# Row sums of the first adjacency: sixteen matmuls in the second network replaced by eight ScalarE sums in the first

## The chip, the cores and the metric

One Trainium2 chip, one core. The kernel is one program on that core; the metric is the device time of one execution in microseconds (us), median of several runs. The kernel before takes 1796.18 us (median of 3 runs, 1793.61 to 1801.1).

## What is computed

Sixteen graphs (batches) of 1024 nodes with 128 features, each with a symmetric 0/1 adjacency matrix, go through two networks, each on a layer-normed and rectified input and with a residual sum. Cut to what matters:

```python
# first network: 4 gated layers, each batch by itself
hw = h @ weight[i]
m  = einsum('bjn,bjd->bnd', adj, hw)          # aggregate
h  = gru_cell(m, h, ...)                      # sigmoid, sigmoid, tanh gates
# second network: 4 convolutions with a batch norm over all batches and nodes
h  = relu(einsum('bnm,bmc->bnc', adj, h @ W[i]) + b[i])
mu, var = mean(h, axis=(0, 1)), var(h, axis=(0, 1))
h  = gamma[i] * (h - mu) * rsqrt(var + 1e-5) + beta[i]
```

The batch norm is an affine map `sc * h + sh` per channel, whose two factors are known only when all sixteen batches of the layer before are done. For batch 0 the kernel does not wait for them: it aggregates the raw features, `adj @ h`, and puts the affine map in afterwards. Since `adj @ (sc*h + sh) = sc*(adj @ h) + sh*(row sums of adj)`, it needs the row sums of the adjacency of batch 0, called `degree`, as one row of 1024 numbers that stands in all 128 partitions.

## The kernel before, in words

The program tests whether the input is exact in a shorter format and runs `exact_path`; `general_path` is the other branch and does not run here.

**First network (about 0 to 1175 us).** Two streams, `sa` (batches 0, 2, 4, ...) and `sb` (1, 3, 5, ...), work in turn. One `half_step(one, two)` (L1035) interleaves the gates of `two` (`gate_step`, L955: 24 matmul instructions at L972) with the aggregation of `one` (`agg_step`, L933, 32 matmuls at L525). Half-steps are counted by `clock`; the first one that is called has the number 3. Tiles of a batch's adjacency stand in SBUF as eight `row` tiles (128 x 1024, fp32r) for all four layers of the batch. Work that is not part of the two streams is put in an agenda with `at(n, place, go)` and comes out in half-step n at one of several places: "late" (L1065) behind the first sigmoid (`first_act`) of the second half of the gates, "gap" (L1078) behind the last gate operation and the split, "mid" and others. `behind` sets only an order on one engine's own queue. From half-step 5 on, the order on TensorE, GpSimd and the DMA queue of SyncE is the written one, and a scheduler orders VectorE and ScalarE within these bounds. In half-step 8 `fetch` (L846) loads the adjacency of batch 2 into `stage` tiles (L573), `glance` (L581) sums their low halves on ScalarE (L587, one sum per tile into a column of `low`), and GpSimd rounds them into new `row` tiles (L578). After a gate step, features go out to DRAM and come back with blocks turned (`cross_h`, L591; `n_h`, L598), and are split in two parts, `ghw` (L905 on ScalarE, L906 on VectorE), which the next aggregation reads.

On GpSimd's DMA queue in half-step 7: a one-column copy that sets the pace (L1054), the 2 MB store of the turned adjacency of batch 1 (L623), and next the rounding casts of half-step 8 (L578).

**Second network (about 1174 to 1780 us).** Per layer and batch: eight loads of the stored bf16 adjacency on the queue of SyncE (L1232), eight casts to `wide` tiles (L1235 on ScalarE, L1237 on VectorE), 32 matmuls at L525. In layer 0 the features y come through GpSimd's queue (L1292) and are split into `chw` (L1294 on ScalarE, L1295 on VectorE); the weights come after the aggregation (`first_weights`, L1298: copy to `cm`, L1304 on ScalarE; matmuls L1305; `conv_done`, L1281). `raw_weights` (L1315) uses `degree` at L1322 once in each of the layers 1, 2 and 3.

`row_sums` (L1326) makes `degree` in layer 0, after the aggregation of batch 0: for each of the eight `wide` tiles and each half, one matmul with a 128 x 128 tile of ones (`ones_r`, made at L1372) as the weights, at L1331, into two PSUM tiles of the pool with two; all 128 rows of the result are the same. Two ScalarE copies (L1335) bring them to `degree`, which lies in `w_mT`, weights that the first network no longer needs.

Of the kernel before, what the change touches and what calls it, by code (L numbers as in the profile page):

```python
# [8 lines left out]
F32 = mybir.dt.float32  # L9
F32R = mybir.dt.float32r  # L10
BF16 = mybir.dt.bfloat16
U16 = mybir.dt.uint16
I32 = mybir.dt.int32
AF = mybir.ActivationFunctionType
ALU = mybir.AluOpType
AX = mybir.AxisListType
P = 128
HALF = 512
# [323 lines left out]
def exact_path(  # L342
# [21 lines left out]
    nc = tc.nc  # L364
    B, N, C = x.shape
    L = g_weight.shape[0]
    NB = N // P
    NH = N // HALF
# [3 lines left out]
    const = ctx.enter_context(tc.tile_pool(name="const", bufs=1))  # L372
    small = ctx.enter_context(tc.tile_pool(name="small", bufs=2))
    dram = ctx.enter_context(tc.tile_pool(name="dram", bufs=1, space=bass.MemoryType.DRAM))
# [7 lines left out]
    def tmp(name):  # L382
        return ps_t.tile([P, HALF], F32, tag="tmp", name=name)

    adjT_d = [dram.tile([NB, P, N], BF16, tag=f"adjT{b}", name=f"adjT_d{b}") for b in range(B)]
    xmid_d = [dram.tile([N, C], F32, tag=f"xmid{b}", name=f"xmid_d{b}") for b in range(B)]
    ymid_d = [dram.tile([P, N], F32, tag=f"ymid{b}", name=f"ymid_d{b}") for b in range(B)]

    def flat(name):
        return keep.tile([P, NB, C], F32, tag="x", name=name, bufs=4)  # L390
# [18 lines left out]
    ones = const.tile([P, 1], F32, tag="ones", name="ones")  # L409
    nc.vector.memset(ones, 1.0)  # L410
    low = const.tile([P, (B + 2) * NB], F32, tag="low", name="low")
    nc.vector.memset(low, 0.0)

    w_c = const.tile([P, L, C], F32, tag="w_c", name="w_c")
    w_mT = const.tile([P, L, 3 * C], F32, tag="w_mT", name="w_mT")
# [50 lines left out]
    def turn_layer(prep, w_g, i):  # L466

        pt = tmp(f"pt_whh{i}")
        for g in range(3):
            nc.tensor.transpose(pt[:, g * P : (g + 1) * P], wns["hh", i][:, g, :], ident)  # L470
        nc.scalar.copy(w_hhT[:, i, :], pt[:, : 3 * P])
        pt = tmp(f"pt_wih{i}")
        for g in range(3):
            nc.tensor.transpose(pt[:, g * P : (g + 1) * P], wns["ih", i][:, g, :], ident)

        w_ihT = prep.tile([P, 3 * C], F32, tag="w_ihT", name=f"w_ihT{i}", bufs=1)
        nc.scalar.copy(w_ihT, pt[:, : 3 * P])
        pg = tmp(f"pt_g{i}")
        nc.tensor.transpose(pg[:, :P], w_g[:, i, :], ident)
        w_gT = prep.tile([P, P], F32, tag="w_gT", name=f"w_gT{i}", bufs=1)  # L480
        nc.scalar.copy(w_gT, pg[:, :P])
        turned[i] = w_gT, w_ihT

    def join_layer(i):
        w_gT, w_ihT = turned[i]
        pw = tmp(f"pt_wm{i}")
        nc.tensor.matmul(pw[:, : 3 * P], w_gT, w_ihT, start=True, stop=True)
        nc.scalar.copy(w_mT[:, i, :], pw[:, : 3 * P])
# [45 lines left out]
    with ExitStack() as st:  # L534
        work = st.enter_context(tc.tile_pool(name="work", bufs=2))
# [45 lines left out]
        def glance(b, stage, js):  # L581

            junk = work.tile([P, N], BF16, tag="junk", name=f"junk{b}_{js[0]}", bufs=1)
            for j in js:
                lows = stage[j % 4].bitcast(U16).rearrange("p (n t) -> p n t", t=2)[:, :, 0]
                k = b * NB + j
                nc.scalar.activation(junk, lows, AF.Copy, accum_out=low[:, k : k + 1])  # L587

        def exchange_out(t, name):
            d = rawd.tile([P, HALF], F32, tag="cross", name=f"cross_{name}", bufs=8)  # L590
            nc.sync.dma_start(d, t)  # L591
            return d
# [19 lines left out]
        def transposes(batches):  # L612

            for b, rows in batches:
                adjT = turned_tile(f"adjT{b}")
                ahead = transpose_rows(b, rows[0], 0, adjT)
                for j in range(NB):
                    go = ahead
                    if j + 1 < NB:
                        ahead = transpose_rows(b, rows[j + 1], j + 1, adjT)  # L620
                    go()
                    yield j
                nc.gpsimd.dma_start(adjT_d[b].rearrange("k p n -> p k n"), adjT)  # L623
                yield NB
# [136 lines left out]
        def behind(*inss):  # L761

            es = ExitStack()
            for ins in () if written[0] else inss:
                es.enter_context(tc.issue_after(ins.ins))
            return es
# [261 lines left out]
        def at(n, place, go):  # L1028
            agenda.setdefault((n, place), []).append(go)

        def due(place):
            for go in agenda.pop((clock[0], place), ()):
                go()

        def half_step(one, two, gated=None, halfway=None):  # L1035

            feed.next_step()
            one.split = []
            if one.i == 0:
                two.fetch()  # L1040
            due("ins")
            if one is sb and one.i == 0 or written[0] and one is sa:
                feed.jobs = transposes([(s.b, s.rows) for s in (sa, sb)])
            if one.i > 0:
                one.split_step()
                two.fetch()
                feed.some(2)
            two.gate_step(0)
            two.half_away(0)
            two.first_four()  # L1050
            if feed.full or (clock[0], "mid") in agenda:

                pace = small.tile([P, 1], F32, tag="pace", name=f"pace{clock[0]}")
                nc.gpsimd.tensor_copy(pace, two.new[:, :1])  # L1054
                feed.store()
                due("mid")
            due("outs")
            one.split_back(0, two.last_act, two.mid_dve)
            one.split_back(1, two.last_act, two.mid_dve)
            if one.i > 0:  # L1060
                feed.some(1)
            two.gate_step(1, None, one.split)
            two.half_away(1)
            with behind(two.first_act):
                due("late")  # L1065
            if one.i == 0:
                feed.some(1)
            two.last_four()
            if gated:
                gated()  # L1070
            if one.i == 0:
                with behind(two.last_m):
                    one.split_step()
            one.agg_step(0)
            if halfway:
                halfway()
            with behind(two.last_act, two.last_dve, *one.split):
                due("gap")  # L1078
            feed.some(NB if written[0] and one is sa else 1)
            one.agg_step(1)  # L1080
            two.finish()
            clock[0] += 1

        sa, sb = Stream(0), Stream(1)
        every = {getattr(mybir.EngineType, e) for e in ("PE", "DVE", "Activation", "Pool", "SP")}
        with tc.tile_pool(name="prep", bufs=1) as prep, tc.manual_schedule(engines=every):
# [22 lines left out]
            late = [[work.tile([P, N], F32, tag="h", name=f"first{j}", bufs=7)] for j in range(4, NB)]  # L1109
# [83 lines left out]

            sa.plan(0)
            sb.plan(1)
            half_step(sa, sb, looks, lambda: turn_layer(prep, w_g, 1))
            join_layer(1)
            half_step(sb, sa, None, lambda: turn_layer(prep, w_g, 2))
# [25 lines left out]
    work = ctx.enter_context(tc.tile_pool(name="work2", bufs=2))  # L1224
# [65 lines left out]
    def first_split(b):  # L1290
        yt = flat(f"y{b}").rearrange("p k c -> p (k c)")
        nc.gpsimd.dma_start(yt, ymid_d[b])  # L1292
        hw = hw_tiles(b, f"chw{b}_0")
        nc.scalar.copy(hw[0], yt)  # L1294
        nc.vector.tensor_sub(hw[1], yt, hw[0].bitcast(F32))  # L1295
        return hw
# [26 lines left out]
            nc.tensor.matmul(pc[hf], w_c[:, i, :], mt[:, cols], start=True, stop=True)  # L1323
        conv_done(0, i, pc, stats)

    def row_sums(rows):  # L1326

        pd = [tmp(f"pt_deg{hf}") for hf in range(NH)]
        for j in range(NB):
            for hf in range(NH):  # L1330
                nc.tensor.matmul(  # L1331
                    pd[hf], ones_r, rows[j][:, hf * HALF : (hf + 1) * HALF], start=(j == 0), stop=(j == NB - 1)
                )
        for hf in range(NH):
            nc.scalar.copy(degree[:, hf * HALF : (hf + 1) * HALF], pd[hf])  # L1335

    xo = []

    def pieces(b):
# [28 lines left out]
            for n0, n in pieces(k):  # L1368
                nc.gpsimd.dma_start(xo_piece(k, n0, n), by_node(xmid_d[k], n0, n))

    ones_r = work.tile([P, P], F32R, tag="ones_r", name="ones_r", bufs=1)
    nc.vector.tensor_copy(ones_r, ones.to_broadcast([P, P]))  # L1372
    degree = w_mT.rearrange("p l c -> p (l c)")[:, :N]

    stats = small.tile([P, B * NH, 6], F32, tag="bn_st", name="stats0")
# [1 line left out]
    for b in range(B):  # L1377
        rows = load_adjT(b, 0)
        hw_next = first_split(b + 1) if b + 1 < B else None
        pm = banks(b, 0)  # L1380
        aggregate(pm, hw, rows, 0)
        if waiting:
            last = first_weights(*waiting, stats)
            if b == 1:
                with tc.issue_after(last.ins):
                    sb.rest()
        if b == B - 1:
            hw_next = raw_split(1)
        aggregate(pm, hw, rows, 1)
        if b == 0:  # L1390
            row_sums(rows)
        hw, waiting = hw_next, (b, pm)


# [1 line left out]
    for i in range(1, L):  # L1396
        rows, pm0, hw0 = load_adjT(0, i), banks(0, i), hw
# [8 lines left out]
        for b in range(1, B):  # L1406
            rows = load_adjT(b, i)
# [28 lines left out]
    for b in range(B):  # L1436
# [3 lines left out]
        for n0, n in pieces(b):  # L1440
# [5 lines left out]
            tag = turns[count % len(turns)]  # L1446
# [60 lines left out]
```

## Time and profile before

| what | value |
|---|---|
| runs shown | 1793.61, 1796.18, 1801.1 us; median 1796.18 |
| the profiled execution | 1796.9 us, of which 1795.0 us span |
| mean granted TensorE clock of it | 0.997 |
| TensorE busy | 98% of the span |
| VectorE, ScalarE, GpSimd busy | 70%, 62%, 22% |

In the page, TensorE stands as PE (matmuls) and PEld (weight loads), VectorE as DVE, ScalarE as ACT, GpSimd as POOL, SyncE's DMA queue as SPq. A line of a timeline gives the start in us from the start of the span, the duration in us, the engine, the line of the kernel, the operation, output <- inputs, shape, count, and in brackets how long the engine sat idle before it and who ended that. A line of a table by stretches gives the busy time of each engine in a stretch of the span, the granted clock, the mean share in which the 16 DMA engines were busy, and their rate.

### The profile page before, as it was taken

The numbers are of one execution on the slowest core, as the hardware profiler recorded it, in microseconds if no ns is written. First come the engines' busy times: TensorE is split into PE (matmuls) and PEld (weight loads), VectorE is DVE, ScalarE is ACT, GpSimd is POOL, SyncE is SP. The second block draws the span as 40 slices with busy tenths as digits, with TensorE's granted clock in tenths as the row PEclk, the third lists the DMA queues.
The fourth block names the chain that finished last, engine by engine and source line by source line (L and its number), as shares of the span: only waits on it lengthen the run. The fifth ranks groups of instructions, "written<-read, shape, count | busy, mean of one in ns | idle before, by whom it ended". The sixth has DMA issues, their size and how long they took to land. (4 is left out here: it accounts for less than half of the span.)

```text
span 1795.0 us, 22286 instructions
## 1 busy us (share of the span) xinstructions
PE 1763.4 (98%) x6742; PEld 1194.0 (67%) x6742; DVE 1258.8 (70%) x2308; ACT 1107.2 (62%) x1717; POOL 389.4 (22%) x417
## 2 busy tenths in 40 slices
PE   9999999999999999999999999999999999999997
PEld 6555565556565556556556555677778888888886
DVE  7567867867776776777786776676666666666665
ACT  5346456556556555755655655477777767768765
POOL 4213322332332331422342333110100000000011
PEclk9999999999999999999999999999999999999999
DMA  7448676776676766766767667778866566767667
GB/s 253 112 125 268 171 223 237 200 207 225 205 211 211 236 191 193 263 197 168 263 185 209 241 194 209 268 277 299 284 223 244 209 244 215 246 223 240 241 220 263
DMA packets 363968, 399.11 MB, mean 222 GB/s; under 512 B 159820, under 2 KB 240496, under 8 KB 363840
## 3 DMA queue, kind: packets, MB, share of 16 engines
q1 hardware_dynamic: 343088, 322.54, 57.1%
q0 software_dynamic: 20224, 74.80, 11.5%
q8 instruction: 55, 0.90, 0.2%
q14 instruction: 73, 0.60, 0.1%
q10 hardware_dynamic: 528, 0.26, 0.0%
HBM read 266.95 MB, written 96.99 MB: 203 GB/s over the span
## 5 line engine op out<-in xcount | busy, mean ns | idle before, releaser
L525 PE MATMUL pm<-row,ghw 128*128 128x512 f32 x2048 | 505.6, 403 | 11.8 <-ACT ghw L905 11.1
L525 PEld LDWEIGHTS pm<-row,ghw 128*128 128x128 f32 x2048 | 384.3, 189 | 124.5 <-issue 26.5
L525 PE MATMUL pc_m<-wide,chw 128*128 128x512 f32 x1024 | 246.1, 396 | 0.0
L609 POOL CAST half<-row 128x1024 bf16<-128x1024 f32 x128 | 148.8, 1171 | 327.2 <-DMA adjT<-half 312.5
L525 PEld LDWEIGHTS pc_m<-wide,chw 128*128 128x128 f32 x1024 | 190.5, 188 | 42.3 <-issue 4.3
L991 ACT ACTIVATE z<-g_z,brz 128x512 f32<-128x512 f32 x128 | 87.5, 684 | 171.3 <-PE g_z L972 171.2
L525 PE MATMUL pc_g_r<-wide,chw 128*128 128x512 f32 x464 | 187.0, 403 | 0.3 <-ACT chw L502 0.3
L578 POOL CAST row<-stage 128x1024 fp32r<-128x1024 f32 x112 | 131.5, 1181 | 243.6 <-DMA stage<-in_adj_dram 221.1
L525 PE MATMUL pc_g_z<-wide,chw 128*128 128x512 f32 x464 | 181.0, 390 | 0.0
L985 DVE SCALAR_TENSOR_TENSOR r<-g_hn,vecs,r 128x512 f32<-128x512 f32 x128 | 95.0, 742 | 118.3 <-ACT r L984 76.6
L1237 DVE CAST wide<-block 128x1024 fp32r<-128x1024 bf16 x160 | 109.8, 692 | 73.2 <-PE pc_m L525 46.2
L1237 DVE CAST wide<-packed 128x1024 fp32r<-128x1024 bf16 x160 | 110.2, 691 | 72.1 <-PE pc_g_z L525 53.9
L944 ACT COPY m<-pm 128x512 f32<-128x512 f32 x128 | 68.5, 586 | 147.9 <-PE pm L525 147.9
L990 ACT ACTIVATE r<-r,vecs 128x512 f32<-128x512 f32 x128 | 91.8, 717 | 104.0 <-DVE r L986 104.0
L997 DVE TENSOR_TENSOR h<-h,r 128x512 f32<-128x512 f32 x96 | 81.8, 852 | 101.6 <-ACT r L990 101.6
L1235 ACT CAST wide<-packed 128x1024 fp32r<-128x1024 bf16 x96 | 100.6, 1048 | 59.1 <-PE pc_m L525 28.3
L972 PE MATMUL g_r<-m,w_mT 128*128 128x512 f32 x256 | 131.5, 595 | 2.8 <-ACT m L944 2.3
L1235 ACT CAST wide<-block 128x1024 fp32r<-128x1024 bf16 x96 | 100.6, 1049 | 52.3 <-PE pc_g_z L525 27.7
L972 PE MATMUL g_xn<-m,w_mT 128*128 128x512 f32 x256 | 130.7, 592 | 0.0
L972 PE MATMUL g_z<-m,w_mT 128*128 128x512 f32 x256 | 130.7, 592 | 0.0
L998 DVE TENSOR_TENSOR h<-h,z 128x512 f32<-128x512 f32 x128 | 118.7, 931 | 4.8 <-ACT z L991 1.9
L1285 DVE BATCH_NORM_STATS2 stats<-feat 128x6 f32<-128x512 f32 x128 | 84.1, 686 | 47.0 <-ACT feat L1284 45.9
(187 smaller groups left out, 2804.3 us busy)
## 6 DMA issues: line engine op xcount, KB each, us to landing
block<-adjT_d SPq DMA_DIRECT2D x256, 256.0 KB, 4.7
packed<-adjT_d SPq DMA_DIRECT2D x256, 256.0 KB, 5.5
stage<-in_adj_dram SPq DMA_DIRECT2D x120, 512.0 KB, 4.8
adjT_d<-adjT POOLq DMA_DIRECT2D x16, 2048.0 KB, 8.3
cross_h<-t_h SPq DMA_DIRECT2D x90, 256.0 KB, 3.2
n_h<-cross_h SPq DMA_DIRECT2D x360, 64.0 KB, 2.0
xmid_d<-x POOLq DMA_DIRECT2D x16, 512.0 KB, 5.4
y<-ymid_d POOLq DMA_DIRECT2D x16, 512.0 KB, 5.9
```

Source lines behind the costliest of these rows:

```text
L525: nc.tensor.matmul(pm[hf], hw[s][:, j * P : (j + 1) * P], rows[j][:, hf * HALF : (hf + 1) * HALF], start=(j == 0 and s == 0), stop=(j == N ...
L578: nc.gpsimd.tensor_copy(t, stage[j % 4])
L609: nc.gpsimd.tensor_copy(t, row.bitcast(F32))
L972: nc.tensor.matmul(po, wT[:, i, g * C : (g + 1) * C], rhs, start=start, stop=stop)
L985: nc.vector.scalar_tensor_tensor(r, phn, b_hn(i), r, ALU.add, ALU.mult)
L990: nc.scalar.activation(r, r, AF.Tanh, bias=b_in(i))
L991: self.last_act = nc.scalar.activation(z, pz, AF.Sigmoid, bias=brz[:, 3 * i + 1 : 3 * i + 2])
L997: nc.vector.tensor_sub(ho, hin, r)
L998: nc.vector.tensor_mul(ho, ho, z)
L1235: nc.scalar.copy(r, t)
L1237: nc.vector.tensor_copy(r, t)
L1285: nc.vector.bn_stats(stats[:, b * NH + hf, :], dst)
```

## The change

The sums of the eight `row` tiles of batch 0 are taken by ScalarE in the first network, one activation (a copy with a sum along the free axis) for each tile, at eight places of the half-steps 5, 6 and 7. A new place "early" is put behind the first sigmoid of the first half of the gates. In the gap of half-step 7 GpSimd's queue stores the 128 x 8 sums to a row of 1024 numbers in DRAM; in the second network, where `row_sums` stood, GpSimd's queue loads that row into all 128 partitions of `degree`. The matmuls, their tile of ones and the two copies are gone. Since the matrix is symmetric, sums along rows and columns are the same.

```diff
+    degree_d = dram.tile([1, N], F32, tag="degree", name="degree_d")
...
+    deg = const.tile([P, NB], F32, tag="deg", name="deg")
...
+        def row_sums(rows, js):
+
+            junk = work.tile([P, N], BF16, tag="junk", name=f"total{js[0]}", bufs=1)
+            for j in js:
+                nc.scalar.activation(junk, rows[j].bitcast(F32), AF.Copy, accum_out=deg[:, j : j + 1])
...
             two.gate_step(0)
+            with behind(two.first_act):
+                due("early")
             two.half_away(0)
...
             sa.plan(0)
             sb.plan(1)
+            places = [(n, place) for n in (5, 6) for place in ("early", "late", "gap")] + [(7, "early"), (7, "late")]
+            for j, (n, place) in enumerate(places):
+                at(n, place, lambda j=j: row_sums(sa.rows, [j]))
+            at(7, "gap", lambda: nc.gpsimd.dma_start(degree_d.rearrange("o (k p) -> p (o k)", p=P), deg))
...
-    def row_sums(rows):
-
-        pd = [tmp(f"pt_deg{hf}") for hf in range(NH)]
-        for j in range(NB):
-            for hf in range(NH):
-                nc.tensor.matmul(
-                    pd[hf], ones_r, rows[j][:, hf * HALF : (hf + 1) * HALF], start=(j == 0), stop=(j == NB - 1)
-                )
-        for hf in range(NH):
-            nc.scalar.copy(degree[:, hf * HALF : (hf + 1) * HALF], pd[hf])
...
-    ones_r = work.tile([P, P], F32R, tag="ones_r", name="ones_r", bufs=1)
-    nc.vector.tensor_copy(ones_r, ones.to_broadcast([P, P]))
...
         if b == 0:
-            row_sums(rows)
+            nc.gpsimd.dma_start(degree, degree_d.rearrange("o n -> (o n)").partition_broadcast(P))
```

## The prediction

> **What bounds the kernel now.** I read first the busy times and the slices of the page, then tables by stretches over the two places that the change touches, then the timelines of TensorE and ScalarE there. The page, first part and the row of PE in 40 slices:
>
> ```profile
> PE 1763.4 (98%) x6742; PEld 1194.0 (67%) x6742; DVE 1258.8 (70%) x2308; ACT 1107.2 (62%) x1717; POOL 389.4 (22%) x417
> ...
> PE   9999999999999999999999999999999999999997
> ```
>
> TensorE has work nearly everywhere, so a matmul that goes is time that goes, unless the next input is late. All waits of TensorE in the trace's list sum to some 21 us; the largest, 11.1 us in 7 waits, is for `ghw` (L905), features on their way back through DRAM, all after 200 us.
>
> The stretches of half-steps 5 to 8 (each starts with its gates):
>
> ```profile
> 85.50:103.00 17.50, 17.50 (x58) 10.52 (x57) 11.97 (x30) 4.78 (x7) 4.90 (x6) 1.00 0.52 128
> 103.00:120.60 17.60, 17.60 (x58) 10.59 (x57) 12.28 (x32) 7.76 (x12) 3.83 (x5) 1.00 0.61 142
> 120.60:138.20 17.60, 17.60 (x57) 10.58 (x57) 10.17 (x18) 11.93 (x22) 1.08 (x2) 1.00 0.45 159
> 138.20:155.80 17.60, 17.60 (x57) 10.57 (x56) 10.56 (x16) 14.15 (x27) 7.09 (x6) 1.00 0.83 270
> ```
>
> The columns after the length are PE, PEld, DVE, ACT, POOL, clock, DMA share, GB/s. TensorE fills all of it at full clock; ScalarE is busy 4.8, 7.8 and 11.9 us of 17.6 where the sums go.
>
> **What is removed.** The timeline of TensorE around the old row sums:
>
> ```profile
> 1185.37 0.39 PE L525 MATMUL pc_g_r<-wide,chw 128*128 128x512 f32 x1
> 1185.78 3.89 PE L1331 MATMUL pt_deg<-wide,ones_r 128*128 128x512 f32 x16
> 1189.51 0.39 PE L525 MATMUL pc_g_z<-wide,chw 128*128 128x512 f32 x1
> ```
>
> A matmul is listed with 0.39 us but they overlap: neighbours at L525 start 0.23 us apart. From 1185.37 to 1189.51 are 4.14 us; without the 16 they would be 0.23. So 3.91 us of TensorE go, not 16 x 0.39 = 6.2. They stand in the middle of a row of matmuls that never pauses, so all 3.91 are on the path, if what follows is in time. The two copies (L1335, 0.95 us together) and the tile of ones (0.29) ran on ScalarE and VectorE beside TensorE: no gain of their own, but they count for the next point.
>
> **What is late next.** Everything after the old sums is wanted 3.9 us sooner. The `wide` tiles follow by themselves: their casts wait for tiles that TensorE frees (1186.51 and 1188.80 on ScalarE waited for L1331 itself). The first use of the next features, `chw` of batch 2, is at 1195.58 and was ready by 1184.7. The tight one is `cm` of batch 1 (L1304), which L1305 reads: copied at 1198.95 to 1199.52, and L1305 began at 1199.66, just when the 18 matmuls before it were through. Now it is wanted at 1199.66 - 3.91 = 1195.75. ScalarE's own queue from 1182.40 to 1199.52 takes 17.12 us, of which 2.17 are idle (0.31, 0.73, 0.29, 0.84), 0.95 are the copies that go, and 0.96 is one `wide` cast that the new order puts before 1182.40 (its tile is now free early). That leaves 13.04 us, ready at 1195.44 and with about 0.2 us of waits that stay (for L1305's first result, and for a tile freed 3.9 us sooner) at 1195.64. Slack 0.1 us. I count 0.1 us lost; bounds 0 and 3.9 (ScalarE sets the pace and the whole gain is gone until it catches up). I take the low end since each term is a row of this timeline.
>
> **What is added on ScalarE.** Eight sums of 128 x 1024. The nearest row is L587, the same operation on other input: 1.05 us and 0.19 for reading the sum, about 1.15 in a row (148.75 to 149.81 to the next start, 1.06). An fp32 input costs the same (L1294, 1.05). The new order on ScalarE puts them where it waits today: behind the sigmoid L984 and before tanh or the other sigmoid. Half-step 5:
>
> ```profile
> 87.41 0.69 ACT L984 ACTIVATE r<-g_r,brz 128x512 f32<-128x512 f32 x1 [1.13 <-PE g_r L972]
> 89.91 0.72 ACT L990 ACTIVATE r<-r,vecs 128x512 f32<-128x512 f32 x1 [1.82 <-DVE r L986]
> ...
> 92.56 0.69 ACT L984 ACTIVATE r<-g_r,brz 128x512 f32<-128x512 f32 x1 [1.03 <-PE g_r L972]
> 95.26 0.72 ACT L990 ACTIVATE r<-r,vecs 128x512 f32<-128x512 f32 x1 [2.02 <-DVE r L986]
> ```
>
> In brackets is the idle time that a sum falls into. The eight are 1.82, 2.02 and (before the copies m at 103.05) 6.37; in half-step 6 1.82, 2.75 and 4.06; in half-step 7 2.37 and 2.18. Each holds 1.24 us. Cost 0; the cover that matters is VectorE's two operations (L985, L986). If a sum took 2.5 us, five of the eight would push the next gate operation by 0.1 to 0.7 us, and VectorE's three operations and the exchange behind it, which end microseconds before TensorE asks. No new table load is in the order. The rows read were written long before, and the next write of these tiles is in half-step 8, after the sums. Bounds 0 and 8 x 1.24 = 9.9 us.
>
> **The store of the sums.** GpSimd's queue gets it behind the 2 MB store at 131.09 (0.89 us to issue). It waits for the eighth sum, at about 130.2, so not at all; issuing 1024 pieces costs about 0.9 us (L743, L540). Behind it on that queue stand the casts of half-step 8, which wait until 147.35 for their data: 15 us of cover. What is left is the DMA engines. The 2 MB take 9.6 us, to 140.7; the small store follows on the same queue: 1024 pieces of 4 bytes, which no row shows. Nearest from below is `n_h` (64 KB in short runs, 1.8 to 2.0 us undisturbed), from above `xmid_d` (512 KB in 1024 runs, 2.9 to 9.3 us, median 4.7). It would be through between 142.6 and 145.4, by the longest at 150. Who cares? The loads of `stage` issued from 143.17 on, which ScalarE awaits with no slack:
>
> ```profile
> 147.25 1.06 ACT L587 ACTIVATE junk<-stage 128x1024 bf16<-128x1024 uint16 x1 [0.76 <-DMA stage<-in_adj_dram]
> ...
> 153.07 3.19 ACT L674 ACTIVATE y_in<-x,ms_in,rs_in 128x128 f32<-128x128 f32 x8
> 156.15 1.05 ACT L944 COPY m<-pm 128x512 f32<-128x512 f32 x2
> ```
>
> From 147.25 to the copies m ScalarE is idle only 0.35 us, and the matmul that reads m starts at 156.78, 0.1 late already. A `stage` load later by d makes TensorE wait d. But between 139.0 and 143.2 the DMA engines are busy only 39%:
>
> ```profile
> 139.00:143.20 4.20, 4.20 (x11) 1.92 (x11) 1.44 (x2) 2.24 (x3) 0.00 (x0) 1.00 0.39 113
> 143.20:147.20 4.00, 4.00 (x10) 1.71 (x9) 2.29 (x4) 2.91 (x5) 0.00 (x0) 1.00 0.87 240
> ```
>
> Twice the pieces of `n_h` at its price are 3.8 us, to 144.5: 1.3 us beside the loads, at half share 0.6. I take 0.5 us; bounds 0 and 2.2 (to 145.4), by the longest row 7. An added transfer cannot speed anything up.
>
> The Trainium skill, page "DMA: Bandwidth & Descriptors", section Bandwidth, speaks against such a transfer: those under 64 KB are dominated by their descriptors, and its Specifications say that pieces under 512 B are read, changed and written back. Its fit for GpSimd's queue, 2.0 us plus bytes over 436 GB/s, gives an estimated 2.0 us; the sum would then be 0.5 us better.
>
> **The load of `degree`.** 512 KB to 128 partitions on the same queue, like y (L1292, 512 KB, 3.4 to 7.0 us). It waits for the last read of `w_mT` as L1369 did before 1137.03 (0.38 us), behind the store at 1135.74; nobody reads it before L1322 at 1334.9. It loads the DMA engines, which are full from 1137 to 1143, by about 1.3 us (512 KB at 378 GB/s); the `ghw` parts at 1151.24 waited for nothing and TensorE wants them at 1155.2. Cost 0, bounds 0 and 1.3.
>
> **Sum.** 1796.9 (the profiled execution) - 3.9 + 0.1 + 0 + 0.5 + 0 = 1793.6 us, 3.3 us or 0.2% less. That execution lay 0.7 us above the median of the runs shown, which themselves spread over 7.5 us; I keep 1793.6. A measurement of this kernel can tell about 0.5%, 9 us, from no change.
>
> **The rivals.**
> - ScalarE becomes the bound at 1195 to 1200: the slack of 0.1 us is thin. Speaks for it: the engine is 92% busy from 1190 to 1200. Against: its list sums to 13.0 us. Costs 1 to 3.9: 1794.5 to 1797.
> - The store meets the `stage` loads: price 2.2 to 3.9 instead of 0.5: 1795.2 to 1797. Also the case in which the change gives nothing.
> - Slower: the 4-byte writes hold the DMA engines for 10 us or more from 140.7 on, across the loads and the exchange of half-step 8. Place: the copies m at 156.15. From a delay of 3.9 us on the change loses; at 10 us it gives 1796.9 - 3.9 + 10 = 1803, and over 13 us it would be measurable. For it: no row has so small pieces; against: the 128-byte runs of `n_h` land in 2 us.
> - More than 3.9: the 7 late exchanges (11.1 us) fall otherwise in the new timing. 1788 to 1792.
>
> **How the numbers follow.** Forecast (1792.4 to 1795) 0.58, ScalarE 0.12, the loads 0.15, slower 0.08, more 0.07. The first three and half of the last two lie within 1789.5 to 1798.5, which also holds a shift of the median by the spread of runs. Faster by over 0.5% only if the exchanges lose nearly all their waits: 0.03; slower by over 0.5% only by a store of over 13 us: 0.05; within: 0.92.
>
> **What the profile of the changed kernel would show.** Matmuls at L525 0.23 us apart through the place where L1331 stood; the eight sums inside idle times of ScalarE and the half-steps still 17.6 us long; the first glance of half-step 8 at most 1 us later within its half-step, the store landing in 2 to 5 us; L1305 for batch 1 without a wait for L1304. I am wrong if TensorE waits over 1 us in half-step 9, or at L1305.

## The result and the profile after

The kernel after takes 1804.53 us (median of 13 runs, 1801.27 to 1807.06), the kernel before on the same chip 1797.28 us (13 runs): ratio 1.0041, 95% interval 1.0033 to 1.0049. It is 7.3 us slower where 3.3 us less were forecast, and outside the range of 1789.5 to 1798.5. The profiled execution has a span of 1801.4 us (before: 1795.0).

The page's busy times and PE row show that little work changed, and where a hole is: one digit 8 in the fourth slice (each is 45 us long, so 135 to 180 us).

```profile
PE 1762.6 (98%) x6726; PEld 1191.5 (66%) x6726; DVE 1253.6 (70%) x2307; ACT 1115.0 (62%) x1731; POOL 384.9 (21%) x419
...
PE   9998999999999999999999999999999999999997
```

The half-steps 5 to 8 as stretches, with the columns of before (length, PE, PEld, DVE, ACT, POOL, clock, DMA share, GB/s):

```profile
85.50:103.00 17.50, 17.50 (x58) 10.52 (x57) 12.37 (x30) 7.83 (x14) 4.20 (x5) 1.00 0.58 137
103.00:120.60 17.60, 17.60 (x58) 10.59 (x57) 12.24 (x32) 10.99 (x18) 4.53 (x5) 1.00 0.64 141
120.60:138.20 17.60, 17.60 (x58) 10.59 (x57) 10.10 (x17) 14.00 (x25) 1.96 (x3) 1.00 0.46 153
138.20:155.80 17.60, 14.75 (x43) 7.58 (x42) 5.87 (x10) 6.48 (x10) 0.22 (x1) 1.00 0.91 115
```

In the first three rows ScalarE has the sums on top (4.8, 7.8 and 11.9 us became 7.8, 11.0 and 14.0) and TensorE still fills its 17.5 and 17.6 us. The fourth row is the failure: TensorE loses 2.9 us, ScalarE has 6.5 us of work instead of 14.2, and the DMA engines are busier than before (0.91 for 0.83) while they move 115 GB/s instead of 270.

The shorter stretches within it, same columns:

```profile
139.00:143.20 4.20, 4.20 (x11) 1.97 (x11) 1.44 (x2) 2.31 (x3) 0.00 (x0) 1.00 1.28 60
143.20:147.20 4.00, 4.00 (x10) 1.72 (x10) 0.69 (x1) 1.29 (x2) 0.00 (x0) 1.00 0.93 37
147.20:151.00 3.80, 1.56 (x4) 0.38 (x2) 0.00 (x0) 0.07 (x1) 0.00 (x0) 1.00 0.54 45
...
160.00:165.00 5.00, 0.34 (x1) 0.00 (x0) 4.23 (x5) 5.00 (x13) 3.08 (x3) 0.89 0.84 302
165.00:170.00 5.00, 4.69 (x6) 2.11 (x7) 5.00 (x6) 2.46 (x5) 2.08 (x2) 0.50 0.64 245
```

Before, the first two of these had shares of 0.39 and 0.87 at 113 and 240 GB/s. The share adds up the time that packets took; 1.28 at 60 GB/s means packets that stay open for long, side by side, while little is moved. A packet of `cross_h` (2 KB) took up to 4.2 us here, before at most 0.2. The last two rows show the end of it: TensorE hardly works from 160 to 165 us, and from 165 to 170 us it works at half clock.

GpSimd's timeline of the kernel after has the store where it was expected:

```profile
131.10 0.89 POOL L631 DMA_DIRECT2D adjT_d<-adjT  x1 [0.34 <-issue]
131.98 0.89 POOL L1209 DMA_DIRECT2D degree_d<-deg  x1
155.58 1.04 POOL L580 CAST row<-stage 128x1024 fp32r<-128x1024 f32 x1 [22.72 <-DMA stage<-in_adj_dram]
```

It landed 18.1 us after its issue, at 150.1 us. SyncE's queue at that time:

```profile
131.81 4.77 SPq L599 DMA_DIRECT2D cross_h<-t_h  x2
136.69 15.01 SPq L606 DMA_DIRECT2D n_h<-cross_h  x8
151.80 10.31 SPq L575 DMA_DIRECT2D stage<-in_adj_dram  x8
```

The eight issues of `n_h` took 5.6 us before; now they take 15.0, because the last of them wait 9.6 us until `cross_h` has landed. The loads of `stage` queue behind them on SyncE and start at 151.8 instead of 143.2 us. ScalarE needs both. Before, it took the features in time:

```profile
144.78 1.12 ACT L905 CAST ghw<-n_h 128x512 fp32r<-128x512 f32 x2
```

and after:

```profile
150.93 0.62 ACT L913 CAST ghw<-n_h 128x512 fp32r<-128x512 f32 x1 [5.99 <-DMA n_h<-cross_h]
153.38 0.62 ACT L913 CAST ghw<-n_h 128x512 fp32r<-128x512 f32 x1 [1.83 <-DMA n_h<-cross_h]
...
155.48 1.06 ACT L589 ACTIVATE junk<-stage 128x1024 bf16<-128x1024 uint16 x1 [0.90 <-DMA stage<-in_adj_dram]
...
157.30 1.06 ACT L589 ACTIVATE junk<-stage 128x1024 bf16<-128x1024 uint16 x1 [0.67 <-DMA stage<-in_adj_dram]
...
161.62 3.17 ACT L682 ACTIVATE y_in<-x,ms_in,rs_in 128x128 f32<-128x128 f32 x8
164.69 1.04 ACT L952 COPY m<-pm 128x512 f32<-128x512 f32 x2
```

The first glance starts at 155.48 instead of 147.25 us, and the copies m, which stand behind the glances on this queue, at 164.69 instead of 156.15, 8.5 us late. Most of this comes from the features: the second cast of `ghw` ends at 154.00 instead of 145.90, 8.1 us late, and from there to the copies m ScalarE waits for `stage` only 1.57 us (0.90 and 0.67; before 0.76 and 0.35). Without any wait for `stage` the copies would still start about 7 us late. TensorE:

```profile
151.60 7.87 PE L527 MATMUL pm<-row,ghw 128*128 128x512 f32 x32 [2.84 <-ACT ghw L913]
159.31 1.02 PE L980 MATMUL g_r<-h,w_hhT 128*128 128x512 f32 x2
165.31 2.07 PE L980 MATMUL g_r<-m,w_mT 128*128 128x512 f32 x2 [4.97 <-ACT m L952]
167.18 1.92 PE L980 MATMUL g_hn<-h,w_hhT 128*128 128x512 f32 x2
...
177.14 3.06 PE L527 MATMUL pm<-row,ghw 128*128 128x512 f32 x11
```

Before, these places stood at 148.13, 155.80, 156.78, 157.74 and 165.92 us. So the delay grows by 3.4 us at the features, by 5.1 us at the copies m ((165.31 - 151.60) - (156.78 - 148.13)), and by 2.7 us in the gates behind them ((177.14 - 165.31) - (165.92 - 156.78)), where a pair of matmuls takes 1.9 to 2.1 us instead of 1.0: **11.2 us** together.

In the second network the gain came as worked out. TensorE around the place of the old row sums:

```profile
1192.44 0.39 PE L527 MATMUL pc_g_r<-wide,chw 128*128 128x512 f32 x1
1192.67 0.39 PE L527 MATMUL pc_g_z<-wide,chw 128*128 128x512 f32 x1
1192.90 0.39 PE L527 MATMUL pc_g_r<-wide,chw 128*128 128x512 f32 x1
...
1201.46 4.24 PE L527 MATMUL pc_m<-wide,chw 128*128 128x512 f32 x18
1205.54 1.04 PE L1319 MATMUL pw_g_hn<-cm,w_c 128*128 128x512 f32 x2
```

The matmuls start 0.23 us apart right through, and L1319 for batch 1 has no wait. From the eighteen matmuls that start at 1188.23 us (before: 1178.42) to this L1319 are 17.31 us, before 21.24: 3.93 us less.

### The profile page after: what moved, and what is told of

The parts are those of the page before. It is cut to its first block, busy times and chain, and to the rows that moved or that the text cites. A ratio compares the mean times of both kernels' runs of the same rounds, so it can differ in the third digit from the quotient of the medians.

```text
span 1801.4 us, 22264 instructions
## 1 busy us (share of the span) xinstructions
PE 1762.6 (98%) x6726; PEld 1191.5 (66%) x6726; DVE 1253.6 (70%) x2307; ACT 1115.0 (62%) x1731; POOL 384.9 (21%) x419
## 5 line engine op out<-in xcount | busy, mean ns | idle before, releaser
L980 PE MATMUL g_z<-m,w_mT 128*128 128x512 f32 x256 | 130.7, 592 | 0.0
L1006 DVE TENSOR_TENSOR h<-h,z 128x512 f32<-128x512 f32 x128 | 114.6, 899 | 4.7 <-ACT z L999 1.4
```

The source lines that it names most:

```text
L980: nc.tensor.matmul(po, wT[:, i, g * C : (g + 1) * C], rhs, start=start, stop=stop)
L1006: nc.vector.tensor_mul(ho, ho, z)
```

## The experiments

Six kernels (e4, e5, e6, e9, e10, e11) were executed once; their total says little, since the runs of one kernel spread over 4 to 10 us. The kernels are read by a local measure from one profiled execution each, the **shift**: start of the aggregation of half-step 9 minus start of that of half-step 7, less the 35.36 us of before (130.56 to 165.92). The kernel after has 177.14 - 130.63 - 35.36 = 11.2 us. "Landing" is from a store's issue to its landing, with the 2 MB store ahead of it unless told otherwise. e3 and e12, the same kernel twice, agree within 0.1 us in both.

### The parts by themselves

Theory: the store of 4-byte pieces alone makes the loss. Rivals: the sums on ScalarE, or the load of `degree`, or the missing matmuls, do.

**e1_sums_only**: neither store nor load.

```diff
-            at(7, "gap", lambda: nc.gpsimd.dma_start(degree_d.rearrange("o (k p) -> p (o k)", p=P), deg))
...
-        if b == 0:
-            nc.gpsimd.dma_start(degree, degree_d.rearrange("o n -> (o n)").partition_broadcast(P))
```

> The changed kernel without both transfers: the eight sums stay on ScalarE and the sixteen matmuls stay away, but nothing is stored or loaded, so that the second network uses old weights in the place of the row sums. If the store of 4-byte pieces is the cause: the whole gain of 3.9 us shows, ratio to before 0.998 (some 1793.5 us where before takes 1797.3), half-steps 8 and 9 last 17.6 us each. If the sums on ScalarE or the new order of the queues were the cause: slower than before, near 1.004.

Measured: 1794.31 us against 1796.49, ratio 0.9991 (0.9981 to 1.0000), span 1791.3 us, shift 0.1 us. With the sums and without the matmuls there is no stall. The median gain is 2.2 us, less than the 3.9 expected; the interval reaches from 0 to 3.4 (see e12).

**e2_store_in_before**: the kernel before, with nothing but the store of a constant tile of the same shape.

```diff
+    degree_d = dram.tile([1, N], F32, tag="degree", name="degree_d")
...
+    deg = const.tile([P, NB], F32, tag="deg", name="deg")
+    nc.vector.memset(deg, 0.0)
...
+            at(7, "gap", lambda: nc.gpsimd.dma_start(degree_d.rearrange("o (k p) -> p (o k)", p=P), deg))
```

> The kernel before with the store alone: a constant 128 x 8 tile goes out in 4-byte pieces at the same place of GpSimd's queue; the sums stay on TensorE. If the store is the cause: it costs what the trace of the changed kernel shows in half-steps 8 and 9, 3.4 + 5.1 + 2.7 = 11.2 us, so some 1808 us, ratio 1.006. If it is the sums, the order or the load: 1.000.

Measured: 1808.32 us against 1796.49, ratio 1.0070 (1.0052 to 1.0087), landing 18.3 us, shift 8.4 us. (The median is 11.8 us up; the profiled execution, the shortest of the four, is at 1805.14.) The store alone, in a kernel that has kept its matmuls, makes the loss; the other parts are not needed for it.

### What makes the pieces slow

Theories: each small piece has a price (count), pieces that share a stretch of DRAM wait for each other (neighbours), the price is that of the target (DRAM). A variant of the second: only neighbours sent from different partitions wait. In e4, e5, e6, e9, e10 and e11 the cuts leave out the lines that drop the load of `degree`.

**e3_runs32**: the same 4 KB as 128 pieces of 32 bytes; the eight numbers of a partition stay together in DRAM, and the reader takes them through a view in that order.

```diff
-    degree_d = dram.tile([1, N], F32, tag="degree", name="degree_d")
+    degree_d = dram.tile([P, NB], F32, tag="degree", name="degree_d")
...
+            at(7, "gap", lambda: nc.gpsimd.dma_start(degree_d, deg))
...
+            mk = mt[:, cols].rearrange("q (k p) -> q k p", p=P)
+            dk = degree.rearrange("q (p k) -> q k p", k=NB)[:, hf * BH : (hf + 1) * BH, :]
+            nc.vector.scalar_tensor_tensor(mk, dk, aff[1], mk, ALU.mult, ALU.add)
```

> The changed kernel with the sums stored as they lie in SBUF: 128 pieces of 32 bytes instead of 1024 of 4, and the vector operation at L1322 reads the row with a stride. If the number of pieces makes the price: about an eighth of 9.4 us, 1.2 us of the DMA engines, in a lull; the stall is gone and some 1793.5 to 1794.5 us, ratio 0.998. If any small write at this place stalls the exchange (by its landing behind the 2 MB store, not by its pieces): still slower than before, 1.002 to 1.004.

Measured: 1794.33 us, ratio 0.9988 (0.9979 to 0.9998), span 1791.4 us, shift 0.2 us. The store needs no change of place, only of layout. The count of pieces and their neighbours changed at once, so the next ones part them.

**e4_half_pieces**: half the numbers.

```diff
+            at(7, "gap", lambda: nc.gpsimd.dma_start(degree_d.rearrange("o (k p) -> p (o k)", p=P)[:, :4], deg[:, :4]))
```

> The store takes only the first four of the eight sums per partition: 512 pieces of 4 bytes instead of 1024, at the same place; the load of `degree` is left out, so the second network uses the old weights as row sums. In the kernel after, the store landed 18.1 us after its issue, 8 to 9 us later than the 2 MB store alone. If each piece has its own price (about 147 ns on each of the 16 engines, 64 pieces per engine): the hold is halved, landing 13 to 14.5 us after issue, TensorE's stall in half-steps 8 and 9 between 0 and 4 us instead of 11.2. If the price is that of the transfer as a whole, whatever its count: landing at 17 to 18.5 us and a stall near 11 us.

Measured: landing 16.4 us, waits of 1.8 and 5.2 us, shift 9.1 us. Neither expectation holds: half the pieces are nearly as slow as all.

**e5_spaced**: all 1024 pieces, 512 bytes apart.

```diff
+    degree_d = dram.tile([N, P], F32, tag="degree", name="degree_d")
...
+            at(7, "gap", lambda: nc.gpsimd.dma_start(degree_d.rearrange("(k p) c -> p k c", p=P)[:, :, 0], deg))
```

> All 1024 pieces of 4 bytes, but each goes to its own row of 512 bytes in DRAM instead of next to its neighbour; the load of `degree` is left out, so the second network uses the old weights as row sums. If a piece is slow since it shares its place in DRAM with neighbours that are being written: landing 10 to 13 us after issue and a stall of 0 to 2 us. If each small piece has its price wherever it goes: landing 17 to 19 us after issue, a stall of 9 to 12 us.

Measured, by the list of what touches `degree_d` in this kernel (issue duration in ns, its place in the span, time to landing):

```profile
L1209 POOL DMA_DIRECT2D degree_d<-deg x1: 888/888/888, 132.0 to 132.0; - x1
...
DMA to landing us min/median/max: 11.0/11.0/11.0
```

One wait of 1.3 us, shift 1.4 us. The same number of pieces of the same size, and 7 us sooner: the count is not what costs most.

**e6_to_sbuf**: the same pieces into a tile of SBUF.

```diff
+    deg2 = const.tile([P, NB, 2], F32, tag="deg2", name="deg2")
...
+            at(7, "gap", lambda: nc.gpsimd.dma_start(deg2[:, :, 0], deg))
```

> The same 1024 pieces of 4 bytes from the same tile, but into a tile of SBUF (each 8 bytes apart) instead of DRAM; the load of `degree` is left out, so the second network uses the old weights as row sums. If writing to DRAM is what makes a piece slow: landing 10 to 12 us after issue (it stands behind the 2 MB store) and no stall. If a piece of 4 bytes is as slow with any target: 17 to 19 us and a stall of 9 to 12 us.

Measured: landing 9.9 us, no stall, shift 0.3 us. These pieces also lie 8 bytes apart, so this run does not part the target from the spacing; e5 shows that DRAM alone does not make pieces slow. (Its one time, 1798.35 us at a span of 1796.6, is not better than before; what it lost lies after 222 us, where it still was 0.4 us ahead of before, and was not followed up.)

**e9_one_line**: 128 pieces, all in one stretch of 512 bytes.

```diff
+            at(7, "gap", lambda: nc.gpsimd.dma_start(degree_d.rearrange("o (k p) -> p (o k)", p=P)[:, :1], deg[:, :1]))
```

> Only the first of the eight sums of each partition is stored: 128 pieces of 4 bytes, all into the same 512 bytes of DRAM; the load of `degree` is left out, so the second network uses the old weights as row sums. Half the pieces had landed only 1.7 us sooner than all (16.4 against 18.1 us), and 1024 pieces set 512 bytes apart landed in 11.0 us. If pieces that fall into the same 512 bytes (or a part of them) are written one after the other, and different stretches side by side, 128 pieces are nearly as slow as 1024: landing 14 to 18 us, stall 2 to 10 us. If the hold grows with the number of pieces and has a fixed part: 512 pieces less give 1.7 us, so 128 land at about 15 us. If instead the count alone decides and the look at 512 pieces was off: 9.5 to 11 us and no stall.

Measured, from the list for `degree_d` of this kernel:

```profile
L1209 POOL DMA_DIRECT2D degree_d<-deg x1: 570/570/570, 132.4 to 132.4; - x1
...
DMA to landing us min/median/max: 15.3/15.3/15.3
```

and from its timeline of TensorE:

```profile
149.38 7.85 PE L527 MATMUL pm<-row,ghw 128*128 128x512 f32 x32 [0.23 <-ACT ghw L913]
...
163.35 2.08 PE L980 MATMUL g_r<-m,w_mT 128*128 128x512 f32 x2 [5.27 <-ACT m L952]
```

Shift 8.2 us. 512 bytes in 128 pieces cost most of what 4 KB in 1024 cost; 4 KB in 128 pieces (e3) cost nothing. The landing fits the first expectation and the second. A fixed part that any store of small pieces pays is excluded by e3, e5 and e6. But among packed stores the hold grows little with the number of stretches of 512 bytes: one, four (e4) and eight (after) landed after 15.3, 16.4 and 18.1 us.

**e10_own_lines**: 1024 pieces, the eight of a partition next to each other.

```diff
+    degree_d = dram.tile([P, NB], F32, tag="degree", name="degree_d")
...
+    deg = const.tile([P, NB, 2], F32, tag="deg", name="deg")
...
+            at(7, "gap", lambda: nc.gpsimd.dma_start(degree_d, deg[:, :, 0]))
```

> All 1024 pieces of 4 bytes into the same 4 KB of DRAM, but in the order of the kernel with 32-byte pieces: the eight numbers of one partition are neighbours, so 512 bytes come from 16 partitions instead of 128; the sums lie 8 bytes apart in SBUF so that no pieces are joined. The load of `degree` is left out, so the second network uses the old weights as row sums. If any pieces that share a stretch of DRAM wait for each other: landing 16 to 19 us, stall 8 to 12 us, as in the kernel after. If only pieces sent by different DMA engines do, and engines serve groups of partitions: landing 10 to 13 us, stall 0 to 3 us.

Measured: landing 18.2 us, waits of 2.9 and 5.0 us, shift 11.7 us. Whether the 128 pieces of a stretch come from 16 partitions or from 128 makes no difference.

**e11_every_16**: 1024 pieces, 16 bytes apart.

```diff
+    degree_d = dram.tile([N, 4], F32, tag="degree", name="degree_d")
...
+            at(7, "gap", lambda: nc.gpsimd.dma_start(degree_d.rearrange("(k p) c -> p k c", p=P)[:, :, 0], deg))
```

> All 1024 pieces of 4 bytes, in the kernel's own order, 16 bytes apart in DRAM (32 pieces in 512 bytes instead of 128); the load of `degree` is left out, so the second network uses the old weights as row sums. If pieces in the same stretch of DRAM go one after the other, the hold is a quarter of the kernel after's 8 to 10 us: landing 10.5 to 13 us, stall 0 to 3 us. If what counts is only whether neighbours share a stretch at all: 17 to 19 us and a stall of 9 to 12 us.

Measured: landing 11.5 us, one wait of 1.9 us, shift 3.7 us, some of it clock (0.91 from 160 to 180 us). With a quarter of the pieces in the same stretch, most of the hold is gone.

In one table (shift and landing in us; pieces in 512 bytes of DRAM):

| kernel | pieces | bytes each | in 512 bytes | landing | shift |
|---|---|---|---|---|---|
| e3 / e12, 32-byte runs | 128 | 32 | 16 | 9.1 / 9.0 | 0.2 / 0.3 |
| e6, to SBUF | 1024 | 4 | - | 9.9 | 0.3 |
| e5, 512 apart | 1024 | 4 | 1 | 11.0 | 1.4 |
| e11, 16 apart | 1024 | 4 | 32 | 11.5 | 3.7 |
| e9, one stretch | 128 | 4 | 128 | 15.3 | 8.2 |
| e4, half | 512 | 4 | 128 | 16.4 | 9.1 |
| after | 1024 | 4 | 128 | 18.1 | 11.2 |
| e10, by partition | 1024 | 4 | 128 | 18.2 | 11.7 |

From 9.1 to 18.1 us of landing are 9.0. Going from 128 pieces of 32 bytes to 1024 of 4 without neighbours takes 1.9 of them (e5); packing the pieces side by side takes the other 7.1. That neighbours matter is shown; how long the shared stretch is, is not, since 4 bytes and 16 bytes apart change the count in any stretch by the same factor.

### Whether another place would do

**e7_store_late**: the store written next to the load, in the second network.

```diff
-            at(7, "gap", lambda: nc.gpsimd.dma_start(degree_d.rearrange("o (k p) -> p (o k)", p=P), deg))
...
         if b == 0:
+            nc.gpsimd.dma_start(degree_d.rearrange("o (k p) -> p (o k)", p=P), deg)
             nc.gpsimd.dma_start(degree, degree_d.rearrange("o n -> (o n)").partition_broadcast(P))
```

> The changed kernel with the same 1024 pieces of 4 bytes stored in the second network, right before the load on GpSimd's queue. If the price is only the place (features and adjacency awaited with no slack in half-step 8): most of it goes and the time is 1793.5 to 1797. If the pieces cost wherever they stand, since the second network also loads all the time: again some us of stall, 1800 to 1806, now at the loads of adjacency blocks.

Measured: 1799.88 us against 1796.49, ratio 1.0021 (1.0009 to 1.0033). It did not test what it was meant to: nothing holds the store back there, so the scheduler issued it as soon as the sums were done, at 130.7 us, ahead of the 2 MB store. From 134 to 139 us the engines moved 11 GB/s, and the 2 MB came later. Its landing took 11.1 us, the shift is 6.4 us. A truly late place was not tried.

**e8_store_early**: all sums in half-steps 5 and 6, the store at the start of half-step 7.

```diff
-            places = [(n, place) for n in (5, 6) for place in ("early", "late", "gap")] + [(7, "early"), (7, "late")]
+            places = [(n, place) for n in (5, 6) for place in ("early", "late", "gap", "gap")]
...
-            at(7, "gap", lambda: nc.gpsimd.dma_start(degree_d.rearrange("o (k p) -> p (o k)", p=P), deg))
+            at(7, "early", lambda: nc.gpsimd.dma_start(degree_d.rearrange("o (k p) -> p (o k)", p=P), deg))
```

> All eight sums are taken in half-steps 5 and 6 (two of them in each gap), so that the same store of 1024 pieces can be issued near 119 us, at the start of half-step 7, far ahead of the 2 MB store and of the loads of `stage`; the rest is the kernel after. If the loss comes from what the store meets (the exchange of half-step 7 and the loads of half-step 8 with no slack): the pieces still hold the engines some 9 us, about 121 to 131, but there only the exchange of half-step 6 is under way, which has some us of slack: stall 0 to 4 us, 1794.3 to 1798 us, ratio 0.998 to 1.001 to the kernel before. If such a store costs its 9 to 11 us wherever it stands: 1803 us or more, ratio 1.004.

Measured: 1800.13 us against 1797.05, ratio 1.0019 (1.0010 to 1.0029), between the two expectations. The store was issued at 119.7 us and landed 12.8 us later, with no other store ahead of it. It meets the `n_h` of half-step 6, which now land after 10.3 to 12.4 us. ScalarE of this kernel:

```profile
133.30 0.62 ACT L913 CAST ghw<-n_h 128x512 fp32r<-128x512 f32 x1 [5.65 <-DMA n_h<-cross_h]
134.19 0.62 ACT L913 CAST ghw<-n_h 128x512 fp32r<-128x512 f32 x1 [0.26 <-DMA n_h<-cross_h]
```

From the aggregation of half-step 6 to that of half-step 9 it loses 4.7 us (57.60 instead of 52.94). The place halves the loss: TensorE's longest wait there is 2.5 us, and no half clock follows it. But the exchange of half-step 6 pays for this store as that of half-step 8 did, and no place was found where a hold of some 10 us met none (e7's place was in effect that of the kernel after).

### The version that beats both

**e12_runs32_again** is e3 once more, with more runs.

> The kernel with 128 pieces of 32 bytes once more, in five rounds, for a narrower interval against the kernel before: without the stall the change's own gain of 3.3 to 3.9 us should stand, ratio 0.998 (0.9975 to 0.999), about 1793.5 us. If the gain is given back elsewhere, as the medians of 2.2 us in two runs hint: ratio 0.9985 to 0.9995.

Measured: 1794.81 us against 1797.43, ratio 0.9988 (0.9979 to 0.9997); with e3, two measurements with the same ratio. It is the fastest complete version here: 2.2 and 2.6 us less than before. The forecast's terms without the store make 3.8 us (3.9 - 0.1), and the intervals reach from 0.4 to 3.8; whether 1 us or so is given back elsewhere is neither shown nor excluded.

## Why the prediction was wrong, point by point

- **The matmuls that go, 3.9 us: right.** TensorE runs through without a gap; from the eighteen matmuls of batch 2 to L1319 there is no wait, and the way there is 3.93 us shorter.
- **What is late next, 0.1 us: right.** The first half of `cm` of batch 1, which L1319 reads first, was copied by 1205.40 us and read at 1205.54.
- **The sums on ScalarE, 0 us: right.** Half-step 5 of the kernel after:

```profile
87.47 0.69 ACT L992 ACTIVATE r<-g_r,brz 128x512 f32<-128x512 f32 x1 [1.13 <-PE g_r L980]
88.06 1.05 ACT L595 ACTIVATE total<-row 128x1024 bf16<-128x1024 f32 x1
89.01 0.19 ACT L595 ACTIVATION_READ_ACCUMULATOR total<-row 128x1 f32 x1
89.99 0.72 ACT L998 ACTIVATE r<-r,vecs 128x512 f32<-128x512 f32 x1 [0.79 <-DVE r L994]
```

  The sum took 1.05 and 0.19 us as taken from L587, and left 0.79 of the 1.82 us idle; the next gate operation starts where it did (89.99, before 89.91), still released by VectorE. e1 confirms it with a shift of 0.1 us.
- **The store of the sums, 0.5 us with bounds 0 and 2.2: this is the step that failed.** Measured: the store was through at 150.1 us, 9.4 after the 140.7 at which the 2 MB had landed before, and cost 11.2 us of TensorE. Two things were wrong in it:
  - The size. The price was "twice the pieces of `n_h`", taken as runs of 128 bytes. In the trace the eight loads `n_h` of an exchange are 1024 packets of 512 bytes, 128 for each load. So 1024 pieces are eight times those of one load, and at its price of 1.9 us they come to an estimated 15 us, a landing at 156 us where the upper bound had 145.4. Nor is it the same work: `n_h` is a load into SBUF, and the new transfer writes 4 bytes side by side into DRAM (e5 shows that the count alone costs only 1.9 us). The other row, `xmid_d`, has runs of 512 bytes too, and the figures taken from it mix stores with loads (the stores alone, L743, took 3.7 to 9.3 us, median 5.4). Neither row has small pieces that share a stretch, so neither is a bound from above. The longest `xmid_d` gave a landing at 150 us, as measured, but by chance; its price of 7 us was named and then left out of the range, as was the Slower rival's 10 us.
  - The path. Only the loads of `stage` were let meet the store. The exchange of half-step 8 met it first. Its `cross_h`, on another queue, kept the issues of `n_h` waiting 9.6 us, and the loads behind them on SyncE. This cost 3.4 us at the features, and since the rest of ScalarE's queue stood behind the late features, it made most of the 5.1 us at the copies m too; the half clock behind that wait cost 2.7.
- **The Slower rival had it**, chance 0.08: "the 4-byte writes hold the DMA engines for 10 us or more from 140.7 on, across the loads and the exchange of half-step 8", 1803 us. It came to 1804.5. What it lacked is the clock: the gates behind the wait of 5 us ran at half rate for 2.7 us. It also put the delay at the loads as much as at the exchange, and its 10 us of hold were a round figure, so a part of the agreement is luck. Its argument against, that the runs of `n_h` land in 2 us, did not bear on it: they are loads in runs of 512 bytes.
- **The load of `degree`, 0 us: right.** It was issued at 1147.7, landed in 9.5 us, and nobody waited for it.
- The sum by spans: +11.2 at half-step 9, of which 9.3 are left at the pace copy near 222 us (222.44 before, 231.71 after), since before has a wait of 1.3 us at 203 us and a clock of 0.83 from 200 to 210, which fall otherwise after; -3.9 in the second network makes 5.4. The span grew by 6.4; the last 1.0 us was not traced.
- The Trainium skill, page "DMA: Bandwidth & Descriptors", section "Anatomy of one DMA — SWDGE (gpsimd) path", had been weighed in the prediction with its fit, an estimated 2.0 us for such a transfer. Measured with nothing ahead of it (e8), the store took 12.8 us; the measurement decides. That page's Specifications say that pieces under 512 bytes are read, changed and written back. Here 1024 such pieces apart from each other landed in 11.0 us and 128 of 32 bytes in 9.1, behind 2 MB: that rule alone does not make 18.1, the neighbours do. A reading by which the write-backs of one stretch wait for each other, and different stretches go side by side, fits the DRAM rows of the table to about 1 us (6.2 us for 128 in a stretch by e9, a quarter of it for e11, and 1.9 for the count give 17.2 for after and 12.6 for e11, measured 18.1 and 11.5), but it is argued, not shown.
- The Trainium skill, page "TensorE: Matmul & The Clock Gate", Part 1, says that the clock falls to half after an idle window of about 3.4 us. The wait of 4.97 us and the 0.50 behind it agree. Shorter waits did both: after 2.84 us the 32 matmuls took 7.87 us, at full rate; in e7, after 2.02 us, they took 9.44 at a clock of 0.66 (151 to 156 us), which the page's figure does not cover; the measurement decides:

```profile
151.14 9.44 PE L527 MATMUL pm<-row,ghw 128*128 128x512 f32 x32 [2.02 <-ACT ghw L913]
```

## What to carry to other kernels

Where a small transfer turns columns into a row, look at its layout in DRAM and not at its bytes: write each partition's numbers as one run and let the reader permute them; here this alone turned +0.41% into -0.12%. When no row of the trace has pieces as small as a new transfer's, the rows there are bound it from below only, and the range must include the case that it slows whatever runs beside it. Ask which transfers are under way at that time on any queue, not only which loads are issued next. Price a delay of inputs by every queue behind it, and add the clock when TensorE is to wait for microseconds.

## What the runs showed of the hardware

- Pieces of 4 bytes side by side in DRAM: 128 of them (512 bytes) landed 6 us later than 128 of 32 bytes (15.3 against 9.1), 48 ns for each if shared out evenly; 1024 of them, in eight stretches, only 9 us later. 1024 of them 512 bytes apart landed after 11.0 us.
- Such a store slows transfers of other queues that touch neither its tile nor its place: `n_h`, 64 KB, landed in up to 13.6 us instead of 4.0, and the 2 MB store ahead of it on its own queue was listed as landed after 18.4 us instead of 9.6. The store's own packets are not long: it went out as 16 packets of 256 bytes, 15 of them at 139 us, each 0.5 us, and as long in e5, where nearly nothing was held. Long were those of the others: up to 4.2 us for one of `cross_h` and 2.7 for one of `n_h`, both 0.2 at most before.
- The busy share of the DMA engines is no measure of what they move: 1.28 at 60 GB/s, with 1.02 at 393 GB/s a few microseconds before in the kernel before (134 to 139 us).
